# Softplus: four terms added on TensorE in PSUM instead of on GpSimd and VectorE

## The chip, the cores and the metric

One core of one Trainium2 chip runs the whole kernel. The metric is the device time of one execution in microseconds. In what follows PE is TensorE, DVE is VectorE, ACT is ScalarE, POOL is GpSimd, SP is the queue that issues DMAs; PEld is the weight load of PE.

## What is computed

Four layers of a selective scan over images, x of 8 x 48 x 48 x 96, each with a residual. After a projection to 192 channels, a 3 x 3 depthwise convolution and silu, each layer scans the 2304 places in four orders (rows or columns, forward or backward) with 16 states a channel:

```python
delta = softplus(dts + dt_proj_b)          # per order, channel, place
def step(h, inp):
    u_t, d_t, b_t, c_t = inp
    dA = exp(d_t[..., None] * A[None])
    h  = dA * h + (d_t * u_t)[..., None] * b_t[:, :, None, :]
    y  = einsum('bkdn,bkn->bkd', h, c_t)   # sum over the 16 states
    return h, y
```

The four orders are added, a layer norm, a gate silu(z) and a projection to 96 channels follow. The fourth layer writes the same recurrence with cumulative sums.

Softplus is computed from v = dts + bias as max(v, 0) + ln(1 + e) + (e - (w - 1)), with e = exp(-|v|) and w the rounded 1 + e; the last bracket gives back what rounding lost in w.

## The kernel before

Two images are a pair, and a layer runs its four pairs one after the other. A pair has twelve groups: three channel tiles t (channels 0 to 127 of either image, and the last 64 channels of both), two phases ph (rows, columns), two directions d. A group has three chunks of 768 places. Layers 0 to 2 so have 3 x 4 x 12 x 3 = 432 chunks. A chunk has 16 units, called states n here: partitions hold 64 channels twice, for two of the 16 states, and two halves of the channels take turns.

For each state, `decay` makes da = exp(delta A) on ACT (L763, three states ahead); `spread` has PE spread the rows of B over the partitions into a PSUM tile b (L666, one state ahead, two tiles b in turn); `scan` multiplies by delta u (L793) and scans (L797) on DVE; POOL multiplies by C (L806); `add_up` has PE add the product into the sum acc (L853, two states behind). Every fourth state (n = 3, 7, 11, 15) is "pooled": its B comes by DMA into a tile bb (`load_b`), POOL multiplies it (`weigh`, L740), DVE only scans, and b holds the decay, so PE spreads nothing for it. C comes by DMA into nine tiles cb.

The main loop in `run` writes one state after the other, and the order of each engine's instructions is that of the program: the spread for the state after; the copy of the carry (L681); the multiply, the scan and POOL's product; then one call of the generator `prepare` for the next chunk and one step of side work (the prologue of the next pair, with its convolutions at L312 and projections at L465, or the epilogue of the last one), and `add_up` for the state two back. At the state where the sum of the chunk before is complete (n = 2) there is no side work; at n = 3 the call and the side work stand ahead of `add_up`, which there begins the new sum with four matmuls (`begin_sum`, L838).

`prepare` works on two halves of 384 places. In each: matmuls with the dt weights into a PSUM bank (L603), six activations on ACT (L608 to L619), two subtractions and additions on POOL (L621, L622), one instruction on DVE that takes the maximum and adds (L625), copies of delta to both halves of the partitions (`to_twins`, L578), the product with u on DVE (`times_u`, L630 or L633), and copies of that. Each `yield` ends one call. Its first call for a chunk is made at n = 15 of the chunk two before, and the next ones at n = 0, 1, 2 and so on; at n = 13 whatever is missing until delta is ready is called at once. Delta and delta u lie in tiles dl and du of two buffers each, the chunk in work and the next one.

PSUM's eight banks are all in use: two for acc, four for the two tiles b, two for everything else (`bank`), of which `prepare` holds one.

In layer 3 a group is one `Edge` of 192 places, with four units of four states; it uses the same `prepare`, and its tile rq has the tag of bb.

Of the kernel before, what the change touches and what calls it, by code (L numbers as in the profile page):

```python
# [39 lines left out]
F32 = mybir.dt.float32  # L40
BF16 = mybir.dt.bfloat16
AF = mybir.ActivationFunctionType
ALU = mybir.AluOpType
# [6 lines left out]
P = 128  # L50
# [29 lines left out]
C_CONVW, C_CONVB, C_DTB, C_ALOG, C_D, C_G, C_B = 0, 9, 10, 14, 78, 82, 83  # L80
# [23 lines left out]
def ss2d_layers_kernel(ctx: ExitStack, tc: tile.TileContext, x_in, consts, weights, out):  # L104
    nc = tc.nc
# [6 lines left out]
    ypool = ctx.enter_context(tc.tile_pool(name="y", bufs=1))  # L112
    rpool = ctx.enter_context(tc.tile_pool(name="brow", bufs=2))
    cbpool = ctx.enter_context(tc.tile_pool(name="cb", bufs=9))
    bbpool = ctx.enter_context(tc.tile_pool(name="bb", bufs=2))
    apool = ctx.enter_context(tc.tile_pool(name="da", bufs=4))
    capool = ctx.enter_context(tc.tile_pool(name="carry", bufs=2))
    gnpool = ctx.enter_context(tc.tile_pool(name="gn", bufs=3))
# [1 line left out]
    sm1 = ctx.enter_context(tc.tile_pool(name="sm1", bufs=1))  # L120
# [10 lines left out]
    ident = cst[:, 0:P]  # L131
    mean_w = cst[:, P : 2 * P]
    group_w = cst[0:DM, 2 * P : 2 * P + DM]
    ones = cpool.tile([P, 1], F32, name="ones")
    nc.gpsimd.memset(ones, 1.0)
    minus = cpool.tile([P, 1], F32, name="minus")
# [136 lines left out]
    def bank():  # L273
        return psum.tile([P, BANK], F32, name="ps", tag="ps")
# [287 lines left out]
    HALF = SCAN // 2  # L562

    def load_dt(c):
        r = layers[c.l].rank
        c.dts = sm1.tile([64, SCAN], F32, name="dts", tag="dts")
        for b in c.batches:
            q0 = 32 * b if c.t == 2 else 0
            nc.sync.dma_start(
                c.dts[q0 : q0 + r, : c.m],  # L570
                state[c.l, c.p]["xd"][c.ph, b, c.d * r : (c.d + 1) * r, c.c0 : c.c0 + c.m],
            )

    def to_twins(z, at, v):

        for g in range(2):
            for h in range(2):
                nc.scalar.copy(z[64 * h : 64 * h + 64, g, at], v[64 * g : 64 * g + 64])  # L578

    def prepare(c):  # L580
        l, p, t, ph, d = c.l, c.p, c.t, c.ph, c.d
        ly, s = layers[l], state[l, p]
        k, r = ph + 2 * d, ly.rank
        dl = ddpool.tile([P, 2, SCAN], F32, name="dl", tag="dl")[:, :, : c.m]
        du = ddpool.tile([P, 2, SCAN], F32, name="du", tag="du")[:, :, : c.m]
        c.dl, c.du = ([z[:, 0], z[:, 1]] for z in (dl, du))
        u = s["u"][t]
        if ph == 1:
            u = u.rearrange("p (h w) -> p w h", w=W)
        if c.dts is None:  # L590
            load_dt(c)
        dts = c.dts
        for z in range(0, c.m, HALF):
            m = min(HALF, c.m - z)
            at = slice(z, z + m)

            ps = bank()
            v = ps[:, :m]
            for b in c.batches:
                q0 = 32 * b if t == 2 else 0  # L600
                o = ps[64 * b : 64 * b + 64] if t == 2 else ps
                chans = slice(P, DIN) if t == 2 else slice(0, P)
                nc.tensor.matmul(  # L603
                    o[:, :m], ly.dtw[q0 : q0 + r, k, chans], dts[q0 : q0 + r, at],
                    start=True, stop=True,
                )
            yield
            nc.scalar.activation(v, v, AF.Identity, bias=ly.column(t, C_DTB + k))  # L608


            e = sm1.tile([P, HALF], F32, name="e", tag="e")[:, :m]
            nc.scalar.activation(e, v, AF.Abs)
            nc.scalar.activation(e, e, AF.Exp, scale=-1.0)
            yield
            lg = sm1.tile([P, HALF], F32, name="lg", tag="lg")[:, :m]
            nc.scalar.activation(lg, e, AF.Ln, bias=ones)
            w1 = sm1.tile([P, HALF], F32, name="w1", tag="w1")[:, :m]
            nc.scalar.activation(w1, e, AF.Identity, bias=ones)  # L618
            nc.scalar.activation(w1, w1, AF.Identity, bias=minus)  # L619
            yield  # L620
            nc.gpsimd.tensor_sub(lg, lg, w1)  # L621
            nc.gpsimd.tensor_add(lg, lg, e)  # L622
            yield
            yield
            nc.vector.scalar_tensor_tensor(v, v, 0.0, lg, ALU.max, ALU.add)  # L625
            yield

            def times_u(o):
                if ph == 0:
                    nc.vector.tensor_mul(o, v, u[:, c.c0 + z : c.c0 + z + m])  # L630
                    return
                r0 = (c.c0 + z) // H
                nc.vector.tensor_mul(  # L633
                    o.rearrange("p (w h) -> p w h", h=H),
                    v.rearrange("p (w h) -> p w h", h=H),
                    u[:, r0 : r0 + m // H, :],
                )

            if isinstance(c, Edge):
                nc.scalar.copy(c.dl[0], v)  # L640
                times_u(c.du[0])
                c.sum_up()
                c.ready = True
                yield
                return

            to_twins(dl, at, v)
            if z + m == c.m:
                if l == NLAYER - 1:
                    c.sum_up()  # L650
                c.ready = True
                yield
            times_u(v)
            yield
            to_twins(du, at, v)
            yield
# [512 lines left out]
    def run(pairs, short):  # L1169
# [50 lines left out]
        rest = Side(rest)  # L1220
        chunks = list(dict.fromkeys(c for _, c, _ in todo))
        drain(prepare(chunks[0]))
        behind = ahead = Side()
        coming = iter(())
# [3 lines left out]
        for k, ((l, p, unit), c, n) in enumerate(todo):  # L1228
# [11 lines left out]
            if k == 0:  # L1240
                coming_to = 1
                coming = prepare(chunks[coming_to])
# [11 lines left out]
            if n == per - 1:  # L1254
                drain(coming)
                if unit + 1 + per == all_units:
                    drain(behind.g)
                    drain(ahead.g)
                coming_to = chunks.index(c) + 2
                coming = prepare(chunks[coming_to]) if coming_to < len(chunks) else iter(())  # L1260
# [140 lines left out]
```

## Time and profile before

| | |
|---|---|
| median of 3 runs | 21473.89 us (21471.84 to 21485.27) |
| profiled execution | 21493.44 us, span 21491.6 us |
| mean granted clock of PE | 0.828 |
| layers 0 to 2 | until about 19550 us |
| layer 3 | about 19600 us to the end |
| POOL, L806 into cb | 6912 instructions, 1811 to 1814 ns each |
| DVE, L797 | 6912 scans, 1733 to 1813 ns each |
| DVE, L793 | 5184 multiplies, 948 ns each |
| ACT, L763 | 6912 exponentials, 900 to 929 ns each |

Busy time is the union of an engine's instructions, so a mean duration times a count can exceed it: the tail of an instruction overlaps the start of the next. Matmuls are pipelined above all. Of the rows in brackets after an instruction, the number is how long its engine sat idle ahead of it, and the name is what released it.

### The profile page before, as it was taken

To read this page: it belongs to the slowest core of one execution; us is meant where nothing else is said; L and a number is where in the kernel's file an instruction comes from. 1 tells how busy PE (TensorE), PEld (TensorE's weight loads), DVE (VectorE), ACT (ScalarE), POOL (GpSimd) and SP (SyncE) were. 2 spreads that over 40 slices of the span, in tenths; PEclk is the share of its full clock that TensorE was granted. 3 is DMA by queue.
4 is the path that set the end of the run, shared out by engine and by line. 5 is a ranking of instruction groups with operands and counts; after the bars stand their busy time and mean duration, and the time that the engine had idled before them with its cause. 6 is when DMAs were issued, how large, how long until landed. Compare 5 with 4: busy or idle time off the path is not lost. (4 is left out here: it accounts for less than half of the span.)

```text
span 21491.6 us, 279915 instructions
## 1 busy us (share of the span) xinstructions
PE 16773.0 (78%) x77186; PEld 6926.1 (32%) x77186; DVE 18848.0 (88%) x15937; ACT 16422.0 (76%) x30026; POOL 17990.6 (84%) x11081
## 2 busy tenths in 40 slices
PE   7787777777887777787777877787777787877886
PEld 2222322322332332332332322332332332334555
DVE  5999999999999999999999999999999999996553
ACT  5777777777777777777777777777777777777776
POOL 5998888888888889889899888888889888886442
PEclk8887887887888887887887888887887887888987
DMA  4777677777677777777777777777777777774221
GB/s 131 195 194 194 188 192 196 188 191 195 187 196 193 188 198 196 187 198 196 189 200 195 187 194 192 188 193 192 189 193 193 187 193 194 187 190 122 80 71 51
DMA packets 1825097, 3858.67 MB, mean 180 GB/s; under 512 B 341808, under 2 KB 692400, under 8 KB 1810352
## 3 DMA queue, kind: packets, MB, share of 16 engines
q1 hardware_dynamic: 1823536, 3840.67, 67.1%
q8 instruction: 636, 10.42, 0.2%
q14 instruction: 925, 7.58, 0.1%
HBM read 3686.90 MB, written 152.27 MB: 179 GB/s over the span
## 5 line engine op out<-in xcount | busy, mean ns | idle before, releaser
L806 POOL TENSOR_TENSOR cb<-cb,da 128x768 f32<-128x768 f32 x5184 | 9344.9, 1814 | 1865.6 <-DVE da L797 555.8
L853 PE MATMUL acc<-cb,twin 128*64 128x384 f32 x27648 | 7360.5, 590 | 100.2 <-POOL cb L806 94.6
L797 DVE TENSOR_TENSOR_SCAN da<-da,carry,b 128x768 f32<-128x768 f32 x3456 | 6267.2, 1813 | 241.4 <-DVE b L793 3.2
L666 PE MATMUL b<-brow,pick 96*64 96x256 bf16 (+2 forms) x22272 | 3407.3, 390 | 3810.5 <-DVE da L797 3387.7
L793 DVE TENSOR_TENSOR b<-du,b 128x768 f32<-128x768 f32 x5184 | 4915.6, 948 | 837.4 <-PE b L666 814.9
L763 ACT ACTIVATE da<-dl,a 128x768 f32<-128x768 f32 x5184 | 4813.0, 929 | 586.3 <-POOL cb L806 516.7
L666 PEld LDWEIGHTS <-pick 96*64 96x64 bf16 x22272 | 1082.9, 122 | 7422.5 <-DVE da L797 5332.8
L740 POOL TENSOR_TENSOR bb<-bb,du 128x768 f32<-128x768 f32 x1728 | 3133.5, 1813 | 138.4 <-DMA bb<-xd 65.8
L806 POOL TENSOR_TENSOR cb<-cb,bb 128x768 f32<-128x768 f32 x1728 | 3129.2, 1811 | 49.3 <-DVE bb L797 30.3
L797 DVE TENSOR_TENSOR_SCAN da<-da,b 128x768 f32<-128x768 f32 x1728 | 3029.8, 1753 | 119.4 <-ACT w L618 0.5
L853 PEld LDWEIGHTS acc<-cb,twin 128*64 128x64 f32 x27648 | 2314.1, 164 | 2259.1 <-issue 1385.9
L578 ACT COPY dl<-ps 64x384 f32<-64x384 f32 x3456 | 1633.5, 473 | 1511.8 <-DVE ps L625 1476.1
L312 PE MATMUL ps<-pad,diag 128*128 128x480 f32 (+1 forms) x4320 | 2290.4, 630 | 8.3 <-DVE eyc L1086 4.0
L763 ACT ACTIVATE b<-dl,a 128x768 f32<-128x768 f32 x1728 | 1555.2, 900 | 748.6 <-DVE da L797 702.5
L797 DVE TENSOR_TENSOR_SCAN bb<-b,carry,bb 128x768 f32<-128x768 f32 x1152 | 2066.2, 1794 | 33.4 <-issue 15.9
L578 ACT COPY du<-ps 64x384 f32<-64x384 f32 x3456 | 1632.8, 472 | 50.8
L603 PE MATMUL ps<-dts,w 6*128 6x384 f32 (+5 forms) x2432 | 1157.4, 718 | 169.0 <-DMA dts<-xd 95.4
L312 PEld LDWEIGHTS ps<-pad,diag 128*128 128x128 f32 x4320 | 718.5, 199 | 1261.1 <-issue 1139.6
L797 DVE TENSOR_TENSOR_SCAN bb<-b,bb 128x768 f32<-128x768 f32 x576 | 998.4, 1733 | 85.7 <-ACT b L763 50.4
L621 POOL TENSOR_TENSOR lg<-lg,w 128x384 f32<-128x384 f32 (+1 forms) x912 | 893.6, 980 | 183.3 <-ACT w L619 183.3
L622 POOL TENSOR_TENSOR lg<-lg,e 128x384 f32<-128x384 f32 (+1 forms) x912 | 890.3, 976 | 71.4
L608 ACT ACTIVATE ps<-ps,w 128x384 f32<-128x384 f32 (+1 forms) x912 | 497.2, 545 | 496.9 <-PE ps L603 488.3
(143 smaller groups left out, 18870.1 us busy)
## 6 DMA issues: line engine op xcount, KB each, us to landing
cb<-xd SPq DMA_DIRECT2D x13952, 192.0 KB
bb<-xd SPq DMA_DIRECT2D x3456, 192.0 KB
brow<-xb SPq DMA_DIRECT2D x864, 72.0 KB
yd<-y SPq DMA_DIRECT2D x48, 1152.0 KB
ey<-yd SPq DMA_DIRECT2D x256, 216.0 KB
cb<-xd SPq DMA_DIRECT2D x128, 384.0 KB
ex<-xs SPq DMA_DIRECT2D x256, 108.0 KB
xd<-xt SPq DMA_DIRECT2D x32, 684.0 KB
```

Source lines behind the costliest of these rows:

```text
L312: nc.tensor.matmul(ps[:, :m], ly.diag[:, int(t == 2), j, :], pad[:, r0 + dy : r0 + dy + nr, dx : dx + W], start=(j == 0), stop=(j == 8),)
L578: nc.scalar.copy(z[64 * h : 64 * h + 64, g, at], v[64 * g : 64 * g + 64])
L603: nc.tensor.matmul(o[:, :m], ly.dtw[q0 : q0 + r, k, chans], dts[q0 : q0 + r, at], start=True, stop=True,)
L621: nc.gpsimd.tensor_sub(lg, lg, w1)
L622: nc.gpsimd.tensor_add(lg, lg, e)
L666: nc.tensor.matmul(o[64 * h : 64 * h + 64], pick[:, b, n : n + 1].to_broadcast([2 * NR, 64]), rows, start=True, stop=True,)
L740: nc.gpsimd.tensor_mul(b, b, self.du[n % 2])
L763: nc.scalar.activation(da, self.dl[n % 2], AF.Exp, scale=layers[self.l].a2[:, int(self.t == 2), n % 2, k, i : i + 1],)
L793: nc.vector.tensor_mul(b, self.du[n % 2], b)
L797: nc.vector.tensor_tensor_scan(way(h), way(da), way(b), start, ALU.mult, ALU.add)
L806: nc.gpsimd.tensor_mul(c, c, h)
L853: nc.tensor.matmul(self.acc[64 * g : 64 * g + 64, a, : self.m // 2], twin, c[:, a, :], start=False, stop=(pair + 2 == NS and not self.turns),)
```

## The change

The bias is taken into the activations that read the PSUM bank, Abs and a new Relu, and the activation that added it in place goes. e, 1 - w, ln(1 + e) and max(v, 0) are kept in the parts of du and dl that the same half will fill later. PE adds the four with matmuls by the identity, two halves of 64 output partitions each, into a new PSUM bank, in two calls of four matmuls; POOL's two instructions and DVE's one go, and with them one call per half. The tiles e, lg and w1 are no longer allocated, and bb gets a third buffer.

```diff
-    bbpool = ctx.enter_context(tc.tile_pool(name="bb", bufs=2))
+    bbpool = ctx.enter_context(tc.tile_pool(name="bb", bufs=3))
...
             yield
-            nc.scalar.activation(v, v, AF.Identity, bias=ly.column(t, C_DTB + k))
-            e = sm1.tile([P, HALF], F32, name="e", tag="e")[:, :m]
-            nc.scalar.activation(e, v, AF.Abs)
+            e, w1, lg, x = du[:, 0, at], du[:, 1, at], dl[:, 0, at], dl[:, 1, at]
+            bias = ly.column(t, C_DTB + k)
+            nc.scalar.activation(e, v, AF.Abs, bias=bias)
+            nc.scalar.activation(x, v, AF.Relu, bias=bias)
             nc.scalar.activation(e, e, AF.Exp, scale=-1.0)
             yield
-            lg = sm1.tile([P, HALF], F32, name="lg", tag="lg")[:, :m]
             nc.scalar.activation(lg, e, AF.Ln, bias=ones)
-            w1 = sm1.tile([P, HALF], F32, name="w1", tag="w1")[:, :m]
             nc.scalar.activation(w1, e, AF.Identity, bias=ones)
-            nc.scalar.activation(w1, w1, AF.Identity, bias=minus)
+            nc.scalar.activation(w1, w1, AF.Identity, bias=ones, scale=-1.0)
             yield
-            nc.gpsimd.tensor_sub(lg, lg, w1)
-            nc.gpsimd.tensor_add(lg, lg, e)
-            yield
-            yield
-            nc.vector.scalar_tensor_tensor(v, v, 0.0, lg, ALU.max, ALU.add)
-            yield
+            v = bank()[:, :m]
+            for i, z1 in enumerate((e, w1, lg, x)):
+                for g in range(2):
+                    half = slice(64 * g, 64 * g + 64)
+                    nc.tensor.matmul(
+                        v[half], ident[:, half], z1, start=(i == 0), stop=(i == 3)
+                    )
+                if i % 2 == 1:
+                    yield
```

## The prediction

> **What bounds the kernel now.** I read the page's busy times first, then the busy times by stretches, the waits by engine, the groups of instructions, and last the timeline of a few chunks.
>
> The page gives the shares of the whole span:
>
> ```profile
> PE 16773.0 (78%) x77186; PEld 6926.1 (32%) x77186; DVE 18848.0 (88%) x15937; ACT 16422.0 (76%) x30026; POOL 17990.6 (84%) x11081
> ```
>
> The stretches (us; busy PE, PEld, DVE, ACT, POOL, each with its count; granted clock; DMA share; GB/s) show that layers 0 to 2 look alike everywhere; this one stands for them:
>
> ```profile
> 10000.00:12000.00 2000.00, 1570.07 (x7112) 613.00 (x7110) 1867.02 (x1498) 1558.40 (x2863) 1787.97 (x1093) 0.83 0.73 194
> ```
>
> DVE is busy 93% there, POOL 89%, PE and ACT 78%. DVE sets the end, POOL is a close second. The decays (L763) start from 204.4 to 19543.2 us, so 432 chunks take 44.8 us each, 2.80 us a state. In layer 3 (from about 19600 us) DVE is half idle. What DVE still waits for:
>
> ```profile
> DVE b L793 <- PE b L666: 814.9, 701, 5.3
> ...
> DVE ps L625 <- POOL lg L622: 270.8, 69, 98.9
> ```
>
> The first row is 1.9 us a chunk: B's rows, spread by PE, come late. Of the second, 134.6 us lie in layer 3 by the waits of that stretch, and the longest, 98.9, at the start, before the loop; 37 us are left for layers 0 to 2. The groups that the change touches, and the nearest one to what it adds (xcount | busy us, mean ns | idle before, releasers):
>
> ```profile
> L853 PE MATMUL acc<-cb,twin 128*64 128x384 f32 x27648 | 7360.5, 590 | 100.2 <-POOL cb L806 94.6 <-DMA cb<-xd 4.2 <-DMA dts<-xd 0.2
> L621 POOL TENSOR_TENSOR lg<-lg,w 128x384 f32<-128x384 f32 (+1 forms) x912 | 893.6, 980 | 183.3 <-ACT w L619 183.3
> L622 POOL TENSOR_TENSOR lg<-lg,e 128x384 f32<-128x384 f32 (+1 forms) x912 | 890.3, 976 | 71.4
> L625 DVE SCALAR_TENSOR_TENSOR ps<-ps,lg 128x384 f32<-128x384 f32 (+1 forms) x912 | 485.7, 533 | 272.3 <-POOL lg L622 270.8 <-ACT ey L1052 1.4
> L612 ACT ACTIVATE e<-ps 128x384 f32<-128x384 f32 (+1 forms) x912 | 439.2, 482 | 33.2 <-POOL lg L622 5.0
> ```
>
> L853 has 27648 records for 13824 matmuls: an fp32 matmul is two records. The timeline (start, us) of two chunks:
>
> ```profile
> 8005.93 2.78 PE L838 MATMUL acc<-y,cst 128*64 128x384 f32 x8
> ...
> 8010.22 0.96 DVE L793 TENSOR_TENSOR b<-du,b 128x768 f32<-128x768 f32 x1 [0.56 <-PE b L666]
> ...
> 8016.50 0.85 PE L666 MATMUL b<-brow,pick 96*64 96x512 bf16 x4 [2.27 <-DVE da L797]
> ...
> 8017.14 1.49 PE L853 MATMUL acc<-cb,twin 128*64 128x384 f32 x4
> ...
> 8029.12 0.52 PE L666 MATMUL b<-brow,pick 96*64 96x512 bf16 x4
> ...
> 8029.47 0.81 PE L853 MATMUL acc<-cb,twin 128*64 128x384 f32 x4
> ...
> 8030.21 1.04 PE L465 MATMUL ps<-u,w 64*96 64x480 f32 x2
> ...
> 8031.21 0.54 DVE L625 SCALAR_TENSOR_TENSOR ps<-ps,lg 128x384 f32<-128x384 f32 x1
> ...
> 8031.66 0.95 DVE L793 TENSOR_TENSOR b<-du,b 128x768 f32<-128x768 f32 x1
> ```
>
> The same four L853 records take 1.49 us at one place and 0.81 at another. Stretches of 2 us tell why (clock after the POOL column):
>
> ```profile
> 8014.00:8016.00 2.00, 0.23 (x1) 0.00 (x0) 1.97 (x2) 1.59 (x5) 2.00 (x2) 1.00 0.93 249
> 8018.00:8020.00 2.00, 2.00 (x6) 0.29 (x4) 1.97 (x3) 1.24 (x4) 2.00 (x2) 0.50 1.05 241
> 8028.00:8030.00 2.00, 2.00 (x12) 0.63 (x10) 1.97 (x3) 0.19 (x1) 1.92 (x3) 1.00 1.05 244
> ```
>
> After PE sat idle its clock is halved for some 3 to 7 us, then full again. PE goes idle at every fourth state, whose B comes from POOL: there it has nothing to spread. Sorted by state, the trace has PE idle 1.3, 1.5, 1.1 and 1.4 us while DVE goes from state 2 to 3, 6 to 7, 10 to 11 and 14 to 15; DVE's waits stand behind the gaps at half clock: 0.9 us before state 1, 0.5 before 5, 0.9 before 9 and 10.
>
> **The change, part by part.** A chunk calls the preparation of the next one once per state, its first call at state 15 of the chunk before; call j falls on state j-2.
>
> VectorE: L625 goes. From its start to the next instruction's are 0.45 us (8031.21 to 8031.66); 864 of them in layers 0 to 2: 389 us, and the 37 us of waits: **-426 us**, all on the engine that sets the end.
>
> GpSimd: 3.9 us a chunk go (980 and 976 ns, twice). DVE's own waits for POOL sum to 10 us, so I count 0 (bounds 0 and -10); it is cover for later only.
>
> ScalarE: six activations before and after. Out go one in place (545 ns at L608) and L612 (482 ns); in come Abs and Relu with a bias, unseen here in this form, between 482 ns and the 607 ns of L619. That is -57 to +171 us of ACT time, on an engine 78% busy, for which DVE waited 66 us at L797: 0, bounds -66 and +66. The ScalarE page of the Trainium skill (ScalarE: Activation LUTs, Rules for kernel authors) says relu, max and add belong on VectorE, which it calls up to three times as fast in bf16. The rows here, fp32 out of PSUM, have 482 ns on ACT against 533 on DVE, so the trace does not agree. By that rule, an estimate: a third of 482 ns, 161 ns of DVE freed 864 times, 139 us instead of 389, and a sum of -105 us instead of the one below. The copies to both halves (L578) waited 1476 us for L625; now they wait for PE, at states 4 and 11 instead of 5 and 13.
>
> TensorE: eight matmuls a half chunk, in two calls of four, hence eight records a call like the 8005.93 row: next start 8008.53, so 2.6 us at half clock, 1.3 at full. 1728 calls: 2.2 to 4.5 ms of PE; with 1.3/0.83 = 1.6 us each 2.7 ms on top of 78% of 19339 us, 92% of it. So it is the place that decides. The calls fall on states 2, 3, 9 and 10.
> - State 2: nothing to spread, no side work; it fills the gap. Cover: 1.3 us idle, and the next spread is needed only after DVE's pooled scan (1.65 us less 0.6). 0 up to 2.3 us.
> - State 3: ahead of the sums' start (L838, 1.3 us) and of the spread for state 5. At full clock PE has 0.35 spread, 1.3 added, 1.0 side work, 1.3 L838, 0.74 L853, 0.52 spread: 5.2 us. DVE meanwhile runs a pooled scan 1.65, a state 2.65 and, now here, the product with u 0.7: 5.0. So 0.2 us of wait; where L838 reads y by columns it stays as slow as at half clock, and 1.5. Today's wait there is 0.5. I take +0.35 a chunk (bounds 0 and 1.3).
> - States 9 and 10: 2.6 us at full clock, 3.1 at the mean, against 1.1 us of idle and 1.05 of lead; part of the rest is made up by an earlier finish at state 8, below. +0.25 (0 and 1.3). PE may wait for L619's successor at state 9; queued behind are that state's L853 and the side work, then the spread for 12.
> - Moved: the second dt matmul from state 7, where it stood ahead of the spread for 9 (8018.56, 1.5 us at half clock), to 6. With two gaps filled and one narrowed, half-clock stretches become fewer. Of 1.9 us of waits I take -0.4 (0 and -1.2).
> Sum for PE: +0.2 us x 432 = **+86 us**.
>
> Buffers: bb gets a third. POOL's waits for bb's loads (66 us at L740) lie off the path: 0. e, w1, lg and x lie in buffers whose last readers are a chunk back: 0. PSUM: the second bank waits at most for an ACT copy of the state before.
>
> Layer 3: 48 edges lose a 0.34 us L625; its wait (134.6 us) is for the chain of activations, which stays; PE can stand behind that chain, 48 x 2 us. A third rq buffer can take away ACT's 68 us. **-15 us**, bounds -150 and +100.
>
> Sum: -426 + 86 - 15 = -355 us. The profiled execution took 21493.4 us (span 21491.6, 1.8 around it), 19.5 above the median of 21473.9; against the median the forecast is **21119, say 21120 us**.
>
> **The rivals.**
> *PE becomes late at states 5 and 12.* For it: 92% of a mean clock, one state of lead, and the ACT wait at state 9. Chunks with L838 in front of that spread already wait longer than those without (0.5 us more, sorted by chunk). If three of the four calls are uncovered at mean clock, less 2.15 us of idle and lead at 10, DVE waits 1.6 + 1.0 = 2.6 us a chunk, less today's 0.5 at state 5: 2.1 x 432 = 907 - 426 = +481: 21955 us. It turns the sign from 0.99 us a chunk on (426/432); half of it gives about 21500. Against: chunks with more PE work are no slower (time and work, over 430 chunks, do not go together). 0.31 for slower.
> *The clock stays full.* If filling the gaps ends most half-clock stretches, the PE waits halve too: -426 - 407 = 20640 us; for it the 2 us stretches, against it the untouched gaps at 7 and 15. 0.12. The Trainium skill (TensorE: Matmul & The Clock Gate, What's actually happening) states that an idle window of about 3.4 us halves the clock and a busy one restores it; the trace agrees in kind, at 0.50 and 1.00.
> *No change:* DVE's free time turns into waits for PE of 0.9 to 1.1 us. 0.07.
> *The change does not do what it says:* Relu could force table loads (1283 ns each). Abs and Identity run here without; 0.01, in slower.
>
> **How the numbers follow.** Forecast 0.49 (20850 to 21400), full clock 0.12, no change 0.07, slower 0.32. Under 0.2% (43 us), about what a measurement of this kernel can tell from no change, is same. The range reaches halfway to the full-clock case, 20720, and past half of the late case, 21780.
>
> **What would show it.** Right: L625, L621, L622 gone; DVE's waits for L666 at 700 to 1000 us; PE near 88 to 92% with a clock of 0.86 or more; L578 waiting for PE, less than 1476 us. Wrong: those waits above 1240 us, with DVE's share below 91%, or a clock unchanged at 0.83.

## The result, and the profile after

The changed kernel takes 21198.92 us (median of 4 runs, 21190.79 to 21234.84); the kernel before, on the same chip, 21479.58. The ratio is 0.9869 (0.9852 to 0.9886). The profiled execution took 21197.61 us, its span 21195.8. The forecast was 21120: faster, as predicted, by 281 us where 355 were expected.

The page's busy times of the changed kernel:

```profile
PE 17667.6 (83%) x91778; PEld 7579.0 (36%) x91778; DVE 18442.2 (87%) x15025; ACT 16372.9 (77%) x30020; POOL 16311.8 (77%) x9257
```

DVE's busy time fell by 406 us, POOL's by 1679, PE's rose by 895 only. The stretch that stood for layers 0 to 2 (busy PE, PEld, DVE, ACT, POOL; then clock, DMA share, GB/s), and four short ones of the same view:

```profile
10000.00:12000.00 2000.00, 1681.49 (x8582) 683.04 (x8580) 1835.17 (x1413) 1567.53 (x2879) 1625.10 (x918) 0.87 0.74 195
...
8012.00:8014.00 2.00, 0.00 (x0) 0.00 (x0) 1.90 (x2) 1.88 (x4) 1.56 (x1) 1.00 1.04 244
8016.00:8018.00 2.00, 2.00 (x10) 0.57 (x10) 1.97 (x2) 0.74 (x3) 2.00 (x3) 0.50 1.04 238
...
8024.00:8026.00 2.00, 1.80 (x14) 0.95 (x16) 2.00 (x3) 1.59 (x4) 1.72 (x1) 1.00 1.02 249
8026.00:8028.00 2.00, 2.00 (x10) 0.47 (x6) 1.97 (x2) 1.95 (x5) 2.00 (x3) 1.00 1.08 249
```

POOL's share fell from 89 to 81%. DVE is down a little, at 92%: it still sets the end, with somewhat more waiting in each chunk. PE has 21% more records in 84% of the stretch, where it was busy for 78% before: its mean clock rose from 0.83 to 0.87, and the new records are shorter than the average one. The short rows show one idle gap (8012 to 8014) with half clock behind it, and stretches from 8024 on, with new matmuls in them, at full clock.

The new groups, and the product with u (xcount | busy, mean ns | idle before, releasers):

```profile
L623 PE MATMUL ps<-du,cst 128*64 128x384 f32 (+1 forms) x7296 | 1399.5, 500 | 76.6 <-ACT du L617 60.3 <-ACT du L613 15.9
L623 PE MATMUL ps<-dl,cst 128*64 128x384 f32 (+1 forms) x7296 | 1335.4, 483 | 0.0
L611 ACT ACTIVATE du<-ps,w 128x384 f32<-128x384 f32 (+1 forms) x912 | 521.1, 571 | 679.1 <-PE ps L603 664.7 <-DVE b L954 2.9 <-DVE da L798 1.7
L612 ACT ACTIVATE dl<-ps,w 128x384 f32<-128x384 f32 (+1 forms) x912 | 515.6, 565 | 0.0
L634 DVE TENSOR_TENSOR ps<-ps,u 128x384 f32<-128x384 f32 x432 | 349.1, 808 | 89.5 <-ACT dl L578 87.4
L631 DVE TENSOR_TENSOR ps<-ps,u 128x384 f32<-128x384 f32 x432 | 236.6, 548 | 201.0 <-ACT dl L578 200.4
```

The identity matmuls take 1399.5 + 1335.4 = 2735 us of PE. Abs and Relu with a bias, for which I had only bounds, take 571 and 565 ns. The last two rows are the surprise. Before, the same product hardly waited for the copies of delta:

```profile
DVE ps L633 <- ACT dl L578: 10.6, 19, 1.4
...
DVE ps L630 <- ACT dl L578: 5.6, 7, 2.3
```

The waits of the changed kernel (us in total, times, longest):

```profile
PE b L667 <- DVE da L798: 2231.9, 1645, 6.6
...
DVE b L794 <- PE b L667: 796.6, 706, 4.1
DVE b L954 <- PE b L667: 314.9, 103, 14.1
ACT dl L578 <- PE ps L623: 294.4, 367, 5.0
DVE ps L631 <- ACT dl L578: 200.4, 85, 103.8
ACT du L578 <- DVE ps L634: 151.8, 223, 2.7
...
DVE ps L634 <- ACT dl L578: 87.4, 95, 3.6
```

The first row was 3387.7 before: PE idles a third less. The wait of DVE for the spread rows (L794) is 797, against 815. Of L631's 200.4 us, 103.8 are a single wait at the start, which stood at L625 before (98.9).

**Where the time went.** From the first decay to the last, layers 0 to 2 took 19339 us before and 19036 now: -303. The rest, layer 3, went from 1948 to 1956: +8. In layers 0 to 2 the changes that I can name are: L625 gone, -389; its waits for POOL within the loop gone, -29; the waits for the spread, -18; the product's waits for the copies of delta (L578), from 12 to 180, +168. They sum to -268; the other 35 us are spread over many small waits that I didn't follow.

Sorted by state, the waits for the spread moved as predicted in place, not in size (us in total, before to after): state 5, 181 to 248; state 12, 0 to 71; states 9 and 10 together, 272 to 25; state 1, 335 to 356. Call the time from the scan before a state to its own scan the passage that leads to it. The share of passages at half clock fell at states 4, 5, 9 and 10 (0.37 to 0.03, 0.28 to 0.01, 0.75 to 0.34, 0.46 to 0.11), and rose at 0, 1 and 2 (0.47 to 0.67, 0.70 to 0.85, 0.41 to 0.50): behind the gaps that the new matmuls fill there is hardly any half clock left, and behind the ones around state 15, which they don't touch, there is more.

Sorted by the clock of their passage, the waits have two kinds. At state 1 the 367 chunks at half clock waited 0.95 us each on average and the 65 at full clock not at all. At state 5 the passage is at full clock in 426 of 432 chunks, and DVE waits 0.57 us there all the same: that wait is not one of the clock, but of what stands ahead of the spread.

### The profile page after: what moved, and what is told of

Same layout as the page of the kernel before. It is cut to its first block, busy times and chain, and to the rows that moved or that the text cites. A ratio compares the mean times of both kernels' runs of the same rounds, so it can differ in the third digit from the quotient of the medians.

```text
span 21195.8 us, 307853 instructions
## 1 busy us (share of the span) xinstructions
PE 17667.6 (83%) x91778; PEld 7579.0 (36%) x91778; DVE 18442.2 (87%) x15025; ACT 16372.9 (77%) x30020; POOL 16311.8 (77%) x9257
## 5 line engine op out<-in xcount | busy, mean ns | idle before, releaser
L807 POOL TENSOR_TENSOR cb<-cb,da 128x768 f32<-128x768 f32 x5184 | 9394.8, 1816 | 3071.2 <-DVE da L798 886.1
L854 PE MATMUL acc<-cb,twin 128*64 128x384 f32 x27648 | 6599.5, 557 | 29.8 <-POOL cb L807 20.5
L794 DVE TENSOR_TENSOR b<-du,b 128x768 f32<-128x768 f32 x5184 | 4906.1, 946 | 813.2 <-PE b L667 796.6
L667 PE MATMUL b<-brow,pick 96*64 96x256 bf16 (+2 forms) x22272 | 3241.2, 371 | 2806.5 <-DVE da L798 2231.9
L854 PEld LDWEIGHTS acc<-cb,twin 128*64 128x64 f32 x27648 | 2068.1, 155 | 1764.6 <-issue 1277.9
L578 ACT COPY dl<-ps 64x384 f32<-64x384 f32 x3456 | 1634.8, 473 | 334.1 <-PE ps L623 294.4
L578 ACT COPY du<-ps 64x384 f32<-64x384 f32 x3456 | 1635.9, 473 | 309.0 <-DVE ps L634 151.8
L623 PE MATMUL ps<-du,cst 128*64 128x384 f32 (+1 forms) x7296 | 1399.5, 500 | 76.6 <-ACT du L617 60.3
L623 PE MATMUL ps<-dl,cst 128*64 128x384 f32 (+1 forms) x7296 | 1335.4, 483 | 0.0
L603 PE MATMUL ps<-dts,w 6*128 6x384 f32 (+5 forms) x2432 | 1035.9, 647 | 146.3 <-DMA dts<-xd 73.8
L611 ACT ACTIVATE du<-ps,w 128x384 f32<-128x384 f32 (+1 forms) x912 | 521.1, 571 | 679.1 <-PE ps L603 664.7
```

Source lines behind the costliest of these rows:

```text
L603: nc.tensor.matmul(o[:, :m], ly.dtw[q0 : q0 + r, k, chans], dts[q0 : q0 + r, at], start=True, stop=True,)
L611: nc.scalar.activation(e, v, AF.Abs, bias=bias)
L623: nc.tensor.matmul(v[half], ident[:, half], z1, start=(i == 0), stop=(i == 3))
L667: nc.tensor.matmul(o[64 * h : 64 * h + 64], pick[:, b, n : n + 1].to_broadcast([2 * NR, 64]), rows, start=True, stop=True,)
L794: nc.vector.tensor_mul(b, self.du[n % 2], b)
L807: nc.gpsimd.tensor_mul(c, c, h)
```

## The experiments

The theory, called A in the expectations, is that of the prediction: DVE sets the end, every wait of DVE counts, and how much PE has to do matters less than where it lies, since an idle gap leaves half clock behind it and makes a later spread late. The rivals are named in each expectation. All times are medians of four runs, and each ratio is to the kernel before on the same chip. "The changed kernel" is 21198.92 us.

**1. The product with u moved off the copies.**

```diff
             to_twins(dl, at, v)
             if z + m == c.m:
                 ...
                 yield
+            else:
+                yield
             times_u(v)
-            yield
+            if z + m == c.m:
+                yield
             to_twins(du, at, v)
```

> In the first half of a chunk the product with u moves one call later than the copies of delta (state 5 instead of 4), the copies of delta u follow in the same call; all else stays. Theory A (the missing term of the sum is that product, which waits 158 us for the copies that ScalarE makes ahead of it): the waits of L631 and L634 for L578 fall under 60 us and the time falls by 100 to 160 us against the changed kernel, to about 21050. Rival B (VectorE then only reaches the multiply of state 5 earlier, for which TensorE is late anyhow): the waits of L794 for L667 grow by as much as the others fall, from 797 to about 900 to 950, and the time stays within 40 us of 21199.

Measured: 21612.88 us, ratio 1.0058 (1.0041 to 1.0074), 414 us slower than the changed kernel. Its waits:

```profile
DVE b L797 <- PE b L670: 1156.2, 931, 5.7
ACT du L578 <- DVE ps L634: 857.9, 371, 5.6
ACT du L578 <- DVE ps L631: 731.2, 373, 5.6
...
DVE ps L631 <- ACT dl L578: 123.1, 13, 103.7
```

DVE's wait for the copies is gone (of the 123.1 all but 19 are the start). But with the product and its copies in one call, ACT reaches the copies while DVE has not yet come to the product, and waits in order for 1589 us in all, with the exponentials and other copies of the next states behind it; the waits for the spread rose with it, to 1156 us. No account that I had gives this size, and the run mixes two edits: it points to a call being needed between copies and their source, and doesn't tell what the wait of the product costs. The question itself is answered by experiment 6.

**2. All eight identity matmuls in PE's gap.** The two calls of four matmuls in a half become one of eight, placed on a state where PE has nothing to spread.

```diff
             yield
+            if z > 0:
+                yield
             v = bank()[:, :m]
...
-                if i % 2 == 1:
+                if i == 3:
                     yield
+            if z == 0:
+                yield
```

> All eight identity matmuls of a half go into one call: state 2 for the first half, state 10 for the second, where TensorE has nothing to spread; states 3 and 9 have none. Theory A (what costs is the place: the four at state 3 stand ahead of the spread that state 5 waits for): the wait ahead of state 5, 248 us now, falls to 100 or less, and the time falls by 100 to 250 us. Rival B (TensorE is short of time as a whole, and the eight in one row make the spread for state 4 or 12 late instead): the waits at 4 and 12, 7 and 71 us now, grow by 150 us or more and the time is the same or longer.

Measured: 21086.92 us, 0.9821 (0.9805 to 0.9837); 112 faster than the changed kernel. DVE's waits in layers 0 to 2:

```profile
DVE b L799 <- PE b L672: 752.1, 729, 4.7
DVE ps L636 <- ACT dl L578: 53.0, 31, 2.2
DVE ps L639 <- ACT dl L578: 46.0, 31, 3.0
```

Sorted by state, the wait for the spread fell at state 5 from 248 to 98 and at 12 from 71 to 40, but rose at 4 from 7 to 153; the product's waits for L578, in layers 0 to 2, fell from 180 to 99. The place of PE's calls has a price, but most of the spread's wait only moved to the state before, since eight matmuls in a row are more than the gap holds. The spread's waits fell by 45 us in all and the product's by 81, so the larger part of this gain is the product's.

**3. Half of the identity matmuls left out.** The terms e and 1 - w are not added.

```diff
             for i, z1 in enumerate((e, w1, lg, x)):
-                for g in range(2):
+                for g in range(2 if i >= 2 else 0):
...
-                        v[half], ident[:, half], z1, start=(i == 0), stop=(i == 3)
+                        v[half], ident[:, half], z1, start=(i == 2), stop=(i == 3)
```

> Leaves out two of the four terms of the sum (e and 1 - w, the correction of rounding), so the calls at states 2 and 9 have no matmul; those at 3 and 10 stay. TensorE loses half of the added work, 1.3 ms at full clock. Theory A (filling the gap at state 2 keeps the clock full behind it, so these matmuls pay for themselves): the clock falls from 0.88 to about 0.86, the wait ahead of state 5 does not fall, and the time stays within 60 us or gets longer. Rival B (added TensorE work is simply a cost of lateness): the waits of L794 for L667 fall by 100 us or more and so does the time.

Measured: 21144.5 us, 0.984 (0.9824 to 0.9857); 54 faster by the medians, 28 by the profiled executions (21169.33). The stretch of layers 0 to 2:

```profile
10000.00:12000.00 2000.00, 1603.31 (x7863) 643.86 (x7862) 1836.64 (x1418) 1571.66 (x2889) 1627.17 (x920) 0.86 0.75 195
```

PE has 719 records less and is busy 78 us less, yet DVE's share is the same to 0.1%. In layers 0 to 2 the waits for the spread fell from 797 to 735 us, the product's rose from 180 to 238. At state 5 the spread's wait did not fall (271 against 248): with the first of the two calls empty, the half-clock share at state 4 is back from 0.03 to 0.28. At state 12, behind the other call that is left empty, the spread's wait fell by about 65 us, to 3. So half of the matmuls is worth little either way: what they cost at state 12 comes back in part at state 5 and in the waits of the product, the latter for a cause that no run shows.

**4. Side work moved into the gaps at states 6 and 14.** One step of side work each is taken from states 3 and 15.

```diff
-                for _ in range(10 if l in short else 0 if ends else 1):
+                for _ in range(10 if l in short else 0 if ends else (1, 1, 1, 0, 1, 1, 2, 1, 1, 1, 1, 1, 1, 1, 2, 0)[n]):
                     side_step(rest) or side_step(behind, ahead)
```

> The step of side work at states 3 and 15, which stands ahead of the spreads for states 5 and 1, moves to states 6 and 14, where TensorE has nothing to spread. Theory A (the remaining 797 us of waits for the spread come from these two places): the waits ahead of states 1 and 5, 356 and 248 us, together fall by 200 us or more and the time by about as much, to 20950 to 21050. Rival B (the waits at state 1 come from the half clock behind the idle time at states 13 to 15, 85% of which passages are at half clock, and one step less hardly helps): the waits fall by under 100 us.

Measured: 20861.44 us, 0.9712 (0.9696 to 0.9728); 337 faster, with a mean clock of 0.896. The wait for the spread:

```profile
DVE b L794 <- PE b L667: 487.8, 553, 4.8
```

By state it fell at 5 from 248 to 91 and at 1 from 356 to 97 (at 0 it rose from 43 to 99). Same work, another place, more gain than the change itself, and more than the 150 to 250 us that A had for it. The clock is only a part of it: the passages to states 1 and 2 are still at half clock in 0.63 and 0.52 of the chunks, and a chunk whose passage to state 1 is at half clock now waits 0.34 us where it waited 0.95, for there is less work ahead of the spread.

**5. More work for PE, of no use.** Six fp32 matmuls by the identity, whose result nobody reads, in the gap at state 14.

```diff
             to_twins(du, at, v)
             yield
+            if z + m == c.m:
+                v = bank()[:, :m]
+                for i in range(3):
+                    for g in range(2):
+                        half = slice(64 * g, 64 * g + 64)
+                        nc.tensor.matmul(
+                            v[half], ident[:, half], s["u"][t][:, :m],
+                            start=(i == 0), stop=(i == 2),
+                        )
```

> Adds six identity matmuls of u into a bank that nobody reads, at state 14, where TensorE has nothing to spread; 2.0 us at full clock. Theory A (states 0 to 2 are late because the idle time at states 13 to 15 halves the clock): the clock rises from 0.88 to 0.90 or more, the waits of L794 for L667 fall from 797 us by 150 us or more, all of it ahead of state 1 (356 us now), and the time falls by about as much though TensorE has more to do. Rival B (more matmuls only make TensorE later): those waits stay or grow, and the time is the same or longer by up to 150 us.

Measured: 20845.14 us, 0.9699 (0.9682 to 0.9715); 354 faster than the changed kernel. First the page's busy times, then the stretch, then DVE's wait for the spread:

```profile
PE 17692.2 (85%) x96962; PEld 7640.4 (37%) x96962; DVE 18405.8 (88%) x15025; ACT 16353.1 (78%) x30020; POOL 16315.2 (78%) x9257
```

```profile
10000.00:12000.00 2000.00, 1700.34 (x9458) 702.74 (x9457) 1885.27 (x1455) 1615.25 (x2968) 1676.86 (x945) 0.95 0.77 201
```

```profile
DVE b L803 <- PE b L676: 472.7, 444, 4.2
```

5184 records more, and PE is busy for only 25 us more, since its clock went from 0.87 to 0.95 in this stretch. The half-clock shares at states 0, 1 and 2 fell from 0.67, 0.85 and 0.50 to 0.07, 0.23 and 0.17, and the wait at state 1 from 356 to 99 us. The 99 chunks that still pass to state 1 at half clock wait 0.97 us each, the 333 at full clock 0.01. That DVE's waits at states 1 and 2 come with half clock behind idle time, and that more work can take them away, is thereby shown. It doesn't hold for all: at state 5, where the clock was full before, the wait is 227 us against 248.

The Trainium skill (TensorE: Matmul & The Clock Gate, Why this matters for your kernels) asks for no gaps over some 3 us. The one ahead of the half-clock stretch at 8016 in the changed kernel is shorter:

```profile
8014.30 0.52 PE L667 MATMUL b<-brow,pick 96*64 96x512 bf16 x4 [2.73 <-DVE da L798]
```

In the three passages ahead of state 15 PE is idle for 0.75, 1.15 and 1.65 us on average, with short work between, though some single gaps there are over 3 us. What decides instead is worked out in the last section.

**6. The product's wait for the copies, without experiment 1's flaw.** Experiment 2's placement frees a call in each half; here it stands between the copies of delta and the product, and the product keeps its own call.

```diff
+            if z > 0:
+                yield
             v = bank()[:, :m]
...
-                if i % 2 == 1:
+                if i == 3:
                     yield
+            if z == 0 and isinstance(c, Edge):
+                yield
...
                 c.ready = True
-                yield
+            yield
             times_u(v)
```

> As e2 (eight matmuls at states 2 and 10), and the first half uses the call that this leaves empty for the copies of delta, at state 3 instead of 4; the product stays at state 4 and the copies of delta u at 5, so no engine's instructions stand behind a wait that they had not before. Theory A (the product's wait for the copies, 158 us in the changed kernel, 78 in e2, is time of VectorE): the waits of L636 and L639 for L578 fall under 30 us and the time falls by 40 to 100 us against e2, to about 21010. Rival B (each wait taken away at state 5 comes back as a wait for the spread): the waits ahead of state 5, 98 us in e2, grow by as much, and the time stays at 21087 within 30 us.

Measured: 21028.97 us, 0.9781 (0.9765 to 0.9797); 58 less than experiment 2, 170 less than the changed kernel. The product's waits:

```profile
DVE ps L636 <- ACT dl L578: 125.9, 12, 103.5
...
DVE ps L639 <- ACT dl L578: 7.1, 8, 2.3
```

Without what lies ahead of the loop, 18.2 of L636's wait are left, so 25 us in all against 99 in experiment 2: 74 us of wait taken away for 58 us of time (27 by the profiled executions), while the waits for the spread went from 752 to 786 us in layers 0 to 2. Against the changed kernel the sum is clearer: the product's waits fell by 155 us and the spread's by 11, and the time by 162 by the profiled executions. This wait, then, is DVE's time, and it comes from the copies standing right ahead of the product.

**7. The places together (4 and 6).**

> e7 with the side steps of e4. If the places add up (theory A), the time is that of e4 less the gain of e7, about 20700 to 20780. If they share one reserve of TensorE's time (rival B), it stays within 50 us of e4's 20861.

Measured: 20738.32 us, 0.9652 (0.9636 to 0.9668), 123 less than experiment 4 where 6 alone gave 170: most of it adds up.

**8. Experiment 4's move on the kernel before.** If the side steps explain the gain by themselves, it must show there too.

```diff
 # on the kernel before
-                for _ in range(10 if l in short else 0 if ends else 1):
+                for _ in range(10 if l in short else 0 if ends else (1, 1, 1, 0, 1, 1, 2, 1, 1, 1, 1, 1, 1, 1, 2, 0)[n]):
```

> The kernel before with the side steps of e4 alone, no identity matmuls. If theory A is right that lateness ahead of states 1 and 5 is a matter of what stands in front of those spreads, and not of the change, its waits for the spread (815 us, of which 335 ahead of state 1 and 181 ahead of state 5) fall by 200 us or more and the time to about 21200 to 21280. Rival B (side work moved to the gap only pays once the identity matmuls keep the clock up): under 100 us.

Measured: 21700.9 us, 1.0098 (1.0081 to 1.0115): 216 slower. A failed for this kernel. A wait of DVE and one of PE:

```profile
DVE b L793 <- PE b L666: 832.8, 631, 5.4
...
PE ps L1011 <- ACT du L578: 140.3, 41, 4.7
```

State 1 gained (335 to 151), but states 0 and 8 lost more (21 to 244, 0 to 125). In sum the waits for the spread are up by 18 us only, so the loss isn't there: of some 205 us more that DVE is idle, 70 are waits of the pooled scans for ACT's decay (66 to 136) and 40 waits of L625 for POOL (271 to 311), and the rest is spread over many. PE now waits for copies out of PSUM ahead of side work (L1011), a row that was not among the larger ones before, and for ACT's copy of y ahead of the new sum (L838) 269 us instead of 80. The kernel before holds one of the two PSUM banks for everything else through state 14, so two side steps there must share the other; in the changed kernel `prepare` is two calls shorter and has given it back. That fits the L1011 row, but no run tests it: argued, not shown.

**9. Two buffers for bb instead of three,** as before the change (`bufs=3` to `bufs=2`).

> The changed kernel with two bb buffers, as before. Theory A (GpSimd and its loads are off the path): the time stays within 40 us of 21199, on either side. Rival B (the third buffer lets the load start earlier, and its want would hold up the SP queue and the C rows behind it): 60 us or more longer, with more waits of L741 for its DMA than 190 us.

Measured: 21196.82 us, 0.986 (0.9844 to 0.9877), the changed kernel's time. The third buffer is worth nothing, as the sum had it.

**10. The sum on POOL, without any identity matmul.** One addition of max(v, 0) and ln(1 + e), without the correction, into a tile in SBUF.

```diff
-            v = bank()[:, :m]
-            for i, z1 in enumerate((e, w1, lg, x)):
...
-                if i % 2 == 1:
-                    yield
+            v = sm1.tile([P, HALF], F32, name="lg", tag="lg")[:, :m]
+            nc.gpsimd.tensor_add(v, lg, x)
+            yield
+            yield
```

> No identity matmuls: GpSimd adds ln(1 + e) and max(v, 0) into a tile of SBUF at states 2 and 9, in one instruction a half; the correction of rounding (e and 1 - w) is left out of the sum. VectorE has no L625, TensorE nothing added. Theory A (VectorE's 389 us are gained in any case, and the matmuls' price is about paid by the clock they keep up): the clock falls back to 0.83 to 0.84, the waits for the spread ahead of state 1 stay near 335 to 356 us, and the time is 21050 to 21250, within 100 us of the changed kernel. Rival B (the added TensorE work has a net price of the sum's bounds): the time is 200 us or more below the changed kernel's, under 21000.

Measured: 21921.89 us, 1.0196 (1.0179 to 1.0213): slower than both kernels, which neither account expected. The groups of the product with u, and the stretch:

```profile
L629 DVE TENSOR_TENSOR lg<-lg,u 128x384 f32<-128x384 f32 x432 | 818.4, 1895 | 225.9 <-ACT dl L578 217.7 <-POOL bb L736 8.1
L626 DVE TENSOR_TENSOR lg<-lg,u 128x384 f32<-128x384 f32 x432 | 712.5, 1649 | 305.5 <-ACT dl L578 303.1 <-POOL bb L736 2.1 <-ACT carry L677 0.3
```

```profile
10000.00:12000.00 2000.00, 1497.47 (x6774) 590.84 (x6776) 1867.47 (x1366) 1523.04 (x2774) 1691.18 (x979) 0.79 0.71 189
```

With delta in SBUF instead of PSUM, the product takes 1895 and 1649 ns instead of 808 and 548: 945 us of DVE in all. By the source view L629 lasts 781 ns at least, 2008 at the median and 4343 at most. The clock is 0.79, lower than before the change: the gaps are open again. The waits for the spread are 561 us, against 797 in the changed kernel; how much of these 236 us is the net price of the identity matmuls can't be read off, because slower products give PE more time too. That price stays open.

**11. Layer 3's edges without the matmuls.** The edges add the terms on POOL, in place in dl, and the copy of delta goes.

```diff
+            if isinstance(c, Edge):
+                for z1 in (w1, e, x):
+                    nc.gpsimd.tensor_add(lg, lg, z1)
+                v = lg
+                yield
+                yield
+            else:
                 v = bank()[:, :m]
                 ...
             if isinstance(c, Edge):
-                nc.scalar.copy(c.dl[0], v)
                 times_u(c.du[0])
```

> In layer 3 alone, GpSimd adds the four terms in place in delta's tile (three instructions), and neither the identity matmuls nor the copy of delta are made there. Theory A (layer 3 came out 8 us longer instead of 15 shorter since TensorE stands behind the chain of activations, 300 us of waits of L954 for the spread there against 207): those waits fall back to 200 to 230 us and layer 3 gets 30 to 100 us shorter. Rival B (layer 3 waits for its chain of activations either way): under 20 us of change, with the waits moved to GpSimd's terms.

Measured: 21133.97 us, 0.983 (0.9813 to 0.9846); 65 faster. Layer 3 takes 1890 us instead of 1956, and its wait for the spread is

```profile
DVE b L960 <- PE b L673: 211.5, 89, 10.8
```

against 314.9 (L954). The product's wait there is for POOL's sum now, 182 us instead of 122 for the copy. In layer 3, where PE stands behind a chain of activations, the identity matmuls and the copy of delta together cost about 65 us more than the three additions on POOL; the run doesn't part the two.

**12. Experiments 5 and 7 together.**

> e8 (eight matmuls at states 2 and 10, copies a state earlier, side steps at 6 and 14) with the six unread matmuls of e5 at state 14. Theory A (e8 took away what stood in front of the spread for state 1; the half clock behind the idle time is still there): the clock rises to 0.93 or more, the waits for the spread fall from 469 us to about 350, and the time to 20580 to 20680. Rival B (both drew on the same 260 us ahead of state 1, 80 of which are left in e8): the time stays within 50 us of 20738.

Measured: 20606.4 us, 0.9584 (0.9568 to 0.96), 132 less than experiment 7, with a clock of 0.929. It is the fastest version, 2.8% below the changed kernel. DVE's wait for the spread:

```profile
DVE b L808 <- PE b L681: 387.3, 402, 4.2
```

## Why the prediction was right, and what was mis-sized

**DVE, -426.** Right: busy time -406, of which 864 instructions of 0.45 us; the waits for POOL in the loop fell by 29 where I had 37. **POOL and bb's third buffer, 0.** Right; POOL lost 1679 us of busy time, and experiment 9 shows the buffer to be worth nothing. **ACT, 0.** Right in sum: Abs and Relu lie between their bounds, there are as many table loads as before, and DVE's waits for the decays in PSUM went from 66 to 49 us in the loop. The wait of L578 for PE is 294 us, far below the 1476 for L625 before.

**PE, +86.** Measured -18, with each part at its place: at state 5 I had +151 and the row says +67; at 12, +108 and it says +71; the relief by less half clock at 9 and 10 I had at -173, and it is -247. The relief was larger where the gaps are filled, but at states 0 to 2 the waits rose by 75, which no step had, and elsewhere by 16. So the relief, 247 less 75, came out at its 173 by two things against each other, and what was mis-sized are the two prices: 259 us together, 138 measured. PE's added load came out at 2735 us, as worked out (2.7 ms), at a clock of 0.87 where 0.86 was asked, but PE is busy for 84% of the stretch and not 92%: the faster clock also shortened all that PE did before.

**The missing term.** I moved the product with u to state 4 and priced its effect on PE's order only. The copies of delta are issued right ahead of it there, and the product is made in place (`ps<-ps,u`): it overwrites the delta that the four copies read, so it can't begin before they are done. That is +168 us, which no step of the sum had; experiment 6 takes nearly all of it away and gets its time back. The forecast is so partly right by luck, one error against another: from -355, with +168 for this wait, -104 for PE, +23 for layer 3, +8 for POOL's waits and -35 unnamed, one is at -295, and the profiled executions differ by 296 (21493.4 to 21197.6).

**Layer 3, -15.** Measured +8, by two larger things against each other: L625's waits for POOL there (134.6 us) are gone, the waits for the spread rose by 96 (219 to 315), the product's wait for the copy (L641) by 107 (15 to 122); 40 us less of waiting for rq (242 to 203) and other small ones make up the rest. I had expected the chain's wait to stay as it was; it came back under other names.

**The rivals.** "PE becomes late" asked for 0.99 us a chunk of new waits; there is none in sum. Its mechanism is there at states 5 and 12, 138 us together, which the relief at 9 and 10 more than pays for. "The clock stays full" was not met, at 0.88 over the span, but experiment 5 shows that its mechanism is there to be had: one more gap filled gives 354 us, more than the change itself. Experiment 12 goes down to 20606 us, below the 20640 that this rival gave, though not by the clock alone (0.929): it also has the earlier copies of experiment 6 and less side work ahead of two spreads.

The prediction's remark on its range has a wrong number: halfway from 21120 to the full-clock case is 20880, not 20720.

**Open.** The net price of the identity matmuls in layers 0 to 2, the rise of half clock around state 15 in the changed kernel, and the cause of experiment 8.

## What to carry to other kernels

Work for an engine whose clock drops after idle gaps isn't priced by its length: ask which gap it falls into and what is late behind that gap, and fill the worst gap first, with work that has to be done anyway or, failing that, with work that has no use. When a step moves, look at every instruction that then touches its PSUM bank just ahead of it: a step that overwrites in place waits for whoever still reads, and that costs as much as a wait for data. An order of side work tuned for one kernel isn't good for its neighbour: experiment 4's table gained 337 us in the one and lost 216 in the other.

## What the runs showed of the hardware

The product of two operands in SBUF, on DVE beside POOL's multiplies of 1816 ns, takes up to 4343 ns where 781 is its least (experiment 10, L629); in the changed kernel, where it reads delta from PSUM, L634 lies between 772 and 871 ns over all 432, with POOL busy for 81% of the stretch beside it. The Trainium skill (SBUF — State Buffer, SBUF: two separate sides) says that DVE, in an instruction with two SBUF inputs, and GpSimd hold their shared ports by an exclusive lock for a whole instruction, the other fully blocked. The trace agrees: 417 of the 432 products of L629 saw an instruction of POOL end while they ran, and all ended 0.66 to 0.77 us behind the last such end, after waiting for one of POOL's (406), two (8) or three (3); the other 15 took 781 to 858 ns.

A matmul whose moving operand was read by columns of the image took twice as long at full clock. In the timeline of the changed kernel, eight records each:

```profile
8024.55 1.46 PE L623 MATMUL ps<-dl,cst 128*64 128x384 f32 x8
...
8025.84 2.74 PE L839 MATMUL acc<-y,cst 128*64 128x384 f32 x8
```

Both are fp32 with 384 columns out of SBUF, and the clock is 1.00 in the stretches that hold them (8024 to 8028 above). The second reads y by columns of the image. L839 by itself shows the same: the starts of a sum that read y by rows at full clock mostly took 1.46 to 1.51 us, those by columns 2.74 to 2.88.

The granted clock of these traces changes only at steps of 3.41 us, and what PE did in one step decides over the next. In layers 0 to 2 of the changed kernel all 378 steps at full clock in which PE was busy for less than 40% were followed by half clock, 263 of 1096 between 40 and 80%, and 2 of 2778 above; the kernel before (526 of 526, 420 of 1482, 0 of 1621) and experiment 5 (211 of 211, 243 of 1303, 0 of 3327) agree. So it isn't the length of one gap that counts, nor need a step be idle, as the prediction had it, but how much of it is idle: of the 643 drops to half clock only 57 stand behind a step in which PE was busy for less than a tenth of it. All 159 steps at half clock in which PE was busy for less than 70% were followed by another.
